# Two graph layers on one core: the first graph's queries as seven products, lead-in copies on VectorE, row sums made with the column sums

## The chip, the cores and the metric

The kernel runs on one core of a Trainium2 chip. The core has a matrix engine (TensorE, PE in the profile), two elementwise engines (VectorE, DVE; ScalarE, ACT), GpSimd (POOL) and SyncE (SP), which here only issues transfers. All data is fp32. The metric is the device time of one launch in microseconds; less is better.

## The reference, cut to what matters

`x` is 16 graphs of 1024 nodes with 256 channels; `adj` is one 1024 x 1024 matrix for all of them. Layer 0, for each graph, with `h = relu(layernorm(x))`:

```python
fea = transpose(h, (0, 2, 1))                    # 256 x 1024
c_adj = mean(fea, axis=1)                        # one number per node
diff = c_adj[:, None, :] - c_adj[:, :, None]
A = abs(abs(sigmoid(diff) - 0.5) - 0.5) * 2.0
Wg = adj * (A + transpose(A)) * 0.5
q = relu((fea @ Wg) * para)                      # "queries", 256 x 1024
k, v = split(h @ kv_w)
x = x + softmax(q k / sqrt(64)) v                # 4 heads
```

Layer 1 takes the sums of the adjacency with the identity added, by rows and by columns, less the diagonal:

```python
deg = sum(A_norm, axis=0) + sum(A_norm, axis=1) - diagonal(A_norm)
A_hat = A_norm * rsqrt(deg)[:, None] * rsqrt(deg)[None, :]
```

It multiplies all graphs with `A_hat` and sends them through two linear layers with batch norms over all graphs.

## The kernel before, in words

**Stages.** A lead-in makes the first graph's keys, values and queries. Then one attention after another runs, of graphs 0 to 15, and each has the next graph's preparation (keys, values, queries) and the earlier graph's layer 1 woven into it as background. A second stage with the second linear layer ends the launch. Every engine does its instructions in the order in which the program lists them: a schedule written out by hand. `weave` (L151) takes a main generator and lets side generators go one step with each of its steps, from a given step on, and runs the sides out after it. `double` (L161) takes two slots of a generator at once. `attention` (L1240) runs 16 steps per graph: the scores of a step are issued (`scores`), ACT takes their Exp (L1089), DVE adds them up (L1113), PE multiplies the step before with the values (L1124), and background steps follow until a budget of PE time is used up. The scores have two PSUM tiles, so PE's next scores wait for the Exps of the last ones.

**Weighting.** `weigh` (L477) makes the weighted adjacency `Wg` in eight tiles of 128 x 1024, each half a row of a 2 x 4 pattern: column half `q`, pair of row blocks `th`. A tile takes two ACT operations (Abs, L508), a third (Tanh, L516) and one on DVE with the adjacency tile (L495). The generator has 17 slots, two per tile, and loads the adjacency one tile ahead into a ring of three buffers (tag "adj"). For graph 0 alone, DVE also reduces each adjacency tile by rows into `rows` (L498), since the sums by rows are needed in layer 1.

**Queries.** `plain_queries` (L638) multiplies all blocks: 32 products of 128 x 128 x 512 in 16 steps, each step two products. It ends each of its four output quarters with one multiplication by `para` (L663) on DVE and a Relu on ACT (L666). `queries` (L537), used for graphs 2 and later, splits both factors into 2 x 2 blocks of quarters and needs seven products of quarters instead of eight (14 steps). For that DVE makes sums and differences: two on the graph's own `h` (`combine`, L534 and L535) and two later (L580, L581), eight on weighted tiles in place (`take`, L571), and nine additions of products out of PSUM (L579 to L605); ACT copies the first product twice. The last quarter is multiplied by `para` two deferrals after the seventh product; `para` tiles have two buffers.

**Keys and values.** `keys_values` (L672) has four steps for keys and four for values; ACT copies each product out of PSUM (L683, L700). `transposed` (L412) turns `h` on PE; ACT copies the result (L430). Three PSUM banks rotate among all of these. `differences` (L456) makes the row of column sums `cbc`: for graph 0 DVE spreads the sums (`columns_of`, L205, L210), PE transposes them and ACT copies them (`broadcast_row`, L216, L222).

**Degrees.** `degrees` (L233) runs in the first attention's background. It first reduces `rows`, then goes over eight strips of the transposed adjacency (128 x 1024, loaded by SP at L226, two ahead, in the same ring "adj"): ACT copies a strip in place and sums it (L241), DVE picks its diagonal (L243, L244). `background(0)` (L964) weaves the steps of graph 1's queries with the weighting from step 0 on, graph 2's norm from 4, the building of seven matrices for layer 1 on GpSimd (`graph`) from 5, and `degrees` from 7.

**The lead-in's end** (L1340 on): transposes and two key products, then the second half of the transposes, `differences(0)`, the other six steps of keys and values with six slots of the weighting, the load of graph 1, the queries of graph 0 with one slot of weighting for each step and graph 1's norm from step 5 on, and the attention.

Of the kernel before, what the change touches and what calls it, by code (L numbers as in the profile page):

```python
# [10 lines left out]
F32 = mybir.dt.float32  # L11
AF = mybir.ActivationFunctionType
ALU = mybir.AluOpType
AX = mybir.AxisListType
# [3 lines left out]
P = 128  # L18
# [5 lines left out]
def gnn_two_layers_kernel(  # L24
# [12 lines left out]
    nc = tc.nc  # L37
    B, N, C = x.shape
    H1 = w1_t.shape[1]
    NT = N // P  # L40
# [3 lines left out]
    FB = 512  # L44
    NH = N // FB
    TH = 2
    NP = NT // TH
# [7 lines left out]
    ident = const.tile([P, P], F32, name="ident")  # L55
# [43 lines left out]
    def layers(shifted):  # L99
# [8 lines left out]
        big = st.enter_context(tc.tile_pool(name=f"big_{kind}", bufs=1))  # L108
        p1 = st.enter_context(tc.tile_pool(name=f"p1_{kind}", bufs=1))
        p2 = st.enter_context(tc.tile_pool(name=f"p2_{kind}", bufs=2))  # L110
        p3 = st.enter_context(tc.tile_pool(name=f"p3_{kind}", bufs=3))
# [11 lines left out]
        xs, hs, hts, ats, qs, ks, vs = {}, {}, {}, {}, {}, {}, {}  # L123
# [20 lines left out]
        def run(*parts):  # L144
            for part in parts:
                while advance(part) is not None:
                    pass
            while queue:
                queue.pop(0)()

        def weave(main, *sides):  # L151

            for i, cost in enumerate(main):
                for start, side in sides:
                    if i >= start:
                        cost += next(side, 0.0)
                yield cost
            for _, side in sides:
                yield from side

        def double(slots):  # L161

            for _ in slots:
                next(slots, None)
                yield 0.0
# [34 lines left out]
        load_x(0)  # L200
        kvw = const.tile([P, CC, 2 * C], F32, tag="kvw", name=f"kvw_{kind}")
        nc.sync.dma_start(out=kvw, in_=kv_w.rearrange("(k p) j -> p k j", p=P))
        rows = big.tile([P, NH, NT], F32, name="rows")

        def columns_of(col, name):  # L205

# [6 lines left out]
                cbs.append(cb)  # L213
            return cbs

        def broadcast_row(dst, cbs, name):  # L216

            for g, cb in enumerate(cbs):
                pt = bank(f"cbp_{name}_{g}")
                for j in range(4):  # L220
                    nc.tensor.transpose(pt[:, j * P : (j + 1) * P], cb[:, j, :], ident)
                nc.scalar.copy(dst[:, g * FB : (g + 1) * FB], pt)  # L222

        def load_adj_t(t, name):
            tile_ = p3.tile([P, N], F32, tag="adj", name=f"{name}_{t}")
            nc.sync.dma_start(out=tile_, in_=adj_t[t * P : (t + 1) * P, :])  # L226
            return tile_

        deg_sm = big.tile([P, 6, NT], F32, name="deg")
        later = {}  # L230
# [1 line left out]

        def degrees():  # L233

            nc.vector.tensor_reduce(row, rows.rearrange("p q t -> p t q"), AX.X, ALU.add)
            ahead = [load_adj_t(t, "at") for t in range(2)]
            yield 0.0
            for t in range(NT):
                a = ahead[t]
                blk = a[:, t * P : (t + 1) * P]  # L240
                nc.scalar.activation(a, a, AF.Copy, accum_out=col[:, t : t + 1])  # L241
                db = p1.tile([P, P], F32, tag="s1", name=f"db_{t}")
                nc.vector.tensor_mul(db, blk, ident)  # L243
                nc.vector.tensor_reduce(diag[:, t : t + 1], db, AX.X, ALU.add)  # L244
                if t + 2 < NT:
                    ahead.append(load_adj_t(t + 2, "at"))
                yield 0.0
            nc.vector.tensor_add(deg, col, row)
            nc.vector.tensor_sub(deg, deg, diag)
            rsqrt(dinv, deg, 1.0, tmp_deg)  # L250
# [161 lines left out]
        def transposed(b, ks, halves=range(NH), meanwhile=None):  # L412

            h = hs["a", b]
            for k in ks:
                if 0 in halves:
                    ht = p3.tile([P, N], F32, tag="ht", name=f"ht_{b}_{k}")
                    hts.setdefault(b, []).append(ht)
            for g in halves:
                pts = [bank(f"htp_{b}_{k}_{g}") for k in ks]  # L420
                for j in range(FB // P):
                    t = g * (FB // P) + j
                    for k, pt in zip(ks, pts):
                        nc.tensor.transpose(
                            pt[:, j * P : (j + 1) * P], h[:, t, k * P : (k + 1) * P], ident
                        )
                    if meanwhile is not None:
                        meanwhile()
                for k, pt in zip(ks, pts):
                    nc.scalar.copy(hts[b][k][:, g * FB : (g + 1) * FB], pt)  # L430

        def squares(b):

# [43 lines left out]
        def weigh(b):  # L477


            csum, cbc = csums[b], cbcs[b]  # L480
            made = weighted[b] = []
            adjs = []

            def load():
                q, th = divmod(len(adjs), NP)
                adjs.append(load_adj(q, th, f"adj_{b}_{q}_{th}"))

            load()
            for slot in range(2 * NH * NP + 1):
                i, odd = divmod(slot, 2)  # L490
                q, th = divmod(i, NP)
                if not odd and i > 0:

                    w, a = made[i - 1], adjs[i - 1]
                    nc.vector.scalar_tensor_tensor(w, w, 1.0, a, op0=ALU.add, op1=ALU.mult)  # L495
                    if b == 0:
                        q, th = divmod(i - 1, NP)
                        nc.vector.tensor_reduce(  # L498
                            rows[:, q, th * TH : (th + 1) * TH], a, AX.X, ALU.add
                        )  # L500
                if not odd and i < NH * NP:
                    q, th = divmod(i, NP)
                    if i + 1 < NH * NP:
                        load()
                    w = p8.tile([P, TH, FB], F32, tag="w", name=f"w_{b}_{q}_{th}")
                    made.append(w)
                    for t in range(TH):
                        nc.scalar.activation(  # L508
                            w[:, t, :].rearrange("p (t q) -> p t q", q=P),
                            cbc[:, q * NT // NH : (q + 1) * NT // NH],  # L510
                            AF.Abs,
                            bias=csum[:, th * TH + t : th * TH + t + 1],
                            scale=-1.0,
                        )
                if odd:
                    nc.scalar.activation(made[i], made[i], AF.Tanh, scale=-0.5 / C)  # L516
                yield 0.0

        AHEAD = 6
# [152 lines left out]
        def keys_values(b):  # L672
            ht = hts[b]
            ks[b] = [p4.tile([P, N], F32, tag="k", name=f"k_{b}_{k}") for k in range(CC)]
            for g in range(NH):
                for j in range(CC):
                    cols = slice(g * FB, (g + 1) * FB)
                    pk = bank(f"pk_{b}_{j}_{g}")
                    for k in range(CC):
                        product(  # L680
                            pk, kvw[:, k, j * P : (j + 1) * P], ht[k][:, cols], k == 0, k == CC - 1
                        )
                    nc.scalar.copy(ks[b][j][:, cols], pk)  # L683
                    yield 1.71

            vs[b] = [p4.tile([P, NT, P], F32, tag="v", name=f"v_{b}_{k}") for k in range(CC)]
            for g in range(NT // 2):
                pv = bank(f"pv_{b}_{g}").rearrange("p (j c) -> p j c", j=2)
                for j in range(2):
                    t = 2 * g + j  # L690
                    for k in range(CC):
                        product(
                            pv[:, j, :],
                            ht[k][:, t * P : (t + 1) * P],
                            kvw[:, k, C : 2 * C],
                            k == 0,
                            k == CC - 1,
                        )
                for k in range(CC):
                    nc.scalar.copy(  # L700
                        vs[b][k][:, 2 * g : 2 * g + 2, :], pv[:, :, k * P : (k + 1) * P]
                    )
                yield 1.71
# [260 lines left out]
        def background(b):  # L964

            if b == 0:
                differences(1)
                for k in range(CC):
# [8 lines left out]
                    (0, w),  # L977
                    (4, norm),
                    (5, islice(build, 8)),
                    (7, islice(sums, 6)),  # L980
                )
                differences(2)
                yield from weave(asked, (0, build), (0, sums))
# [328 lines left out]
        with st:  # L1312
# [22 lines left out]
            else:  # L1335
# [20 lines left out]
                run(islice(products, 2))  # L1356
                transposed(0, range(CC), (1,))
                differences(0)
                run(weave(products, (0, islice(weighers[0], AHEAD))))
                load_x(1, True)  # L1360
                run(weave(plain_queries(0), (0, weighers[0]), (5, Norm(1, True).all())))
                load_x(2, True)
                attention()
                attn.close()
# [348 lines left out]
```

## Time and profile before

| | |
|---|---|
| time, median of 3 runs | 2460.47 us (2459.99 to 2460.54) |
| the profiled execution | 2460.34 us |
| its span | 2458.6 us, granted clock 0.993 |
| busy in the span | PE 98%, DVE 82%, ACT 51%, POOL 23% |
| weighting, per tile | ACT 2 x 0.716 and 1.06 us, DVE 1.22 us |
| rows of the adjacency, L498 | 8 x 1.213 us on DVE |
| k copies L683, v copies L700, ACT | 0.58 us, 0.377 us each |
| strips, L241, ACT | 8 x 1.05 us, and 0.19 us for the sum |

A timeline row has the start, the length, the engine, the line, the operation, out<-in, shapes, a count, and in brackets how long the engine was idle before it and who released it. A table of stretches has each engine's busy time with its number of instructions. A wait table has who waited for whom. PE's instructions come in pairs for each product of 64 columns; a step of 1.71 us shows as eight of them.

### The profile page before, as it was taken

The numbers are of one execution on the slowest core, as the hardware profiler recorded it, in microseconds if no ns is written. First come the engines' busy times: TensorE is split into PE (matmuls) and PEld (weight loads), VectorE is DVE, ScalarE is ACT, GpSimd is POOL, SyncE is SP. The second block draws the span as 40 slices with busy tenths as digits, with TensorE's granted clock in tenths as the row PEclk, the third lists the DMA queues.
The fourth block names the chain that finished last, engine by engine and source line by source line (L and its number), as shares of the span: only waits on it lengthen the run. The fifth ranks groups of instructions, "written<-read, shape, count | busy, mean of one in ns | idle before, by whom it ended". The sixth has DMA issues, their size and how long they took to land. (4 is left out here: it accounts for less than half of the span.)

```text
span 2458.6 us, 35932 instructions
## 1 busy us (share of the span) xinstructions
PE 2412.4 (98%) x13290; PEld 832.6 (34%) x13290; DVE 2003.9 (82%) x3103; ACT 1257.7 (51%) x1870; POOL 559.5 (23%) x645
## 2 busy tenths in 40 slices
PE   9999999999999999999999999999999999999994
PEld 4333333333333333333333333333333332334444
DVE  5678888988888888888898888888888878767775
ACT  7874554545464545445454546454454534335554
POOL 1381202111111212020211212121202103136652
PEclk9999999999999999999999999999999999999997
DMA  4675545363645554453536355544545353456559
GB/s 146 204 242 182 172 138 179 118 229 125 209 139 193 171 189 163 158 171 126 209 117 231 120 201 160 197 164 167 172 134 188 116 201 142 152 197 230 196 193 372
DMA packets 204553, 437.18 MB, mean 178 GB/s; under 512 B 21456, under 2 KB 96720, under 8 KB 200272
## 3 DMA queue, kind: packets, MB, share of 16 engines
q1 hardware_dynamic: 173328, 327.29, 39.7%
q0 software_dynamic: 31040, 107.50, 11.6%
q8 instruction: 107, 1.75, 0.3%
q14 instruction: 78, 0.64, 0.1%
HBM read 331.36 MB, written 103.35 MB: 177 GB/s over the span
## 5 line engine op out<-in xcount | busy, mean ns | idle before, releaser
L1089 ACT ACTIVATE p<-sc 128x1024 f32<-128x1024 f32 x512 | 495.4, 1020 | 649.5 <-PE sc L1081 649.5
L1113 DVE TENSOR_TENSOR acc<-acc,p 128x1024 f32<-128x1024 f32 x384 | 469.8, 1223 | 58.2 <-ACT p L1089 36.9
L1081 PE MATMUL sc<-q,k 64*64 64x512 f32 x4096 | 498.6, 602 | 0.5 <-ACT p L1089 0.5
L1124 PE MATMUL o<-p,v 128*64 128x512 f32 x2048 | 494.7, 604 | 0.0
L174 PE MATMUL pa<-aht,h_b 128*64 128x512 f32 x1536 | 346.0, 592 | 1.1 <-ACT h_b L368 1.1
L174 PE MATMUL pg<-w,x_h 128*64 128x512 f32 x1472 | 332.0, 592 | 0.0
L1081 PEld LDWEIGHTS sc<-q,k 64*64 64x64 f32 x4096 | 131.5, 132 | 336.4 <-issue 287.8
L1124 PEld LDWEIGHTS o<-p,v 128*64 128x64 f32 x2048 | 124.6, 136 | 297.7 <-issue 251.2
L1142 POOL DMA_DIRECT2D out_d<-os x58 | 32.9, 568 | 803.2 <-DVE os L1138 803.2
L495 DVE SCALAR_TENSOR_TENSOR w<-w,adj 128x1024 f32<-128x1024 f32 x128 | 164.9, 1288 | 46.1 <-ACT w L516 45.1
L174 PEld LDWEIGHTS pa<-aht,h_b 128*64 128x64 f32 x1536 | 110.1, 137 | 220.6 <-issue 207.8
L174 PEld LDWEIGHTS pg<-w,x_h 128*64 128x64 f32 x1472 | 105.7, 137 | 210.1 <-issue 198.4
L508 ACT ACTIVATE w<-cbc,csum 128x512 f32<-128x512 f32 x256 | 170.3, 716 | 0.0
L516 ACT ACTIVATE w<-w 128x1024 f32<-128x1024 f32 x128 | 135.6, 1059 | 2.5
L571 DVE TENSOR_TENSOR w<-w,w 128x1024 f32<-128x1024 f32 x112 | 134.6, 1232 | 1.5
L174 PE MATMUL pv<-kvw_f,ht 128*64 128x256 f32 x1024 | 116.1, 379 | 0.0
L174 PE MATMUL pk<-ht,kvw_f 128*64 128x512 f32 x512 | 115.2, 593 | 0.2 <-ACT ht L430 0.2
L174 PE MATMUL py<-at,w 128*64 128x512 f32 x464 | 112.6, 593 | 0.8 <-DVE at L729 0.7
L174 PE MATMUL py<-at,w1s 128*64 128x512 f32 x448 | 107.9, 595 | 0.0
L1453 ACT ACTIVATE yin_f<-yin_f,sm_f 128x512 f32<-128x512 f32 x128 | 93.5, 803 | 19.0 <-DMA yin_f<-y_d 17.0
L826 POOL DMA_DIRECT2D y_d<-y x112 | 61.6, 550 | 145.1 <-DVE y L846 75.8
L1160 DVE TENSOR_REDUCE part<-acc 128x16 f32<-128x512 f32 x128 | 87.8, 686 | 4.4
(197 smaller groups left out, 2968.6 us busy)
## 6 DMA issues: line engine op xcount, KB each, us to landing
aht<-aht_d SPq DMA_DIRECT2D x224, 512.0 KB
adj<-in_adj_dram SPq DMA_DIRECT2D x128, 512.0 KB
y_d<-y POOLq DMA_DIRECT2D x128, 256.0 KB, 3.0
yin_f<-y_d SPq DMA_DIRECT2D x32, 1024.0 KB
para<-in_para_dram SPq DMA_DIRECT2D x64, 256.0 KB
x_d<-x_x POOLq DMA_DIRECT2D x16, 1024.0 KB, 5.1
xo_f<-x_d SPq DMA_DIRECT2D x32, 512.0 KB
out_dram<-xo_f POOLq DMA_DIRECT2D x32, 512.0 KB, 11.1
```

The source lines that it names most:

```text
L174: nc.tensor.matmul(dst[r], left[:, r], right, start=start, stop=stop)
L495: nc.vector.scalar_tensor_tensor(w, w, 1.0, a, op0=ALU.add, op1=ALU.mult)
L508: nc.scalar.activation(w[:, t, :].rearrange("p (t q) -> p t q", q=P), cbc[:, q * NT // NH : (q + 1) * NT // NH], AF.Abs, bias=csum[:, th * ...
L516: nc.scalar.activation(made[i], made[i], AF.Tanh, scale=-0.5 / C)
L571: nc.vector.tensor_sub(block(i)[part], block(x)[part], block(y)[part])
L826: nc.gpsimd.dma_start(out=y1_d[i][:, j, :], in_=y)
L1081: nc.tensor.matmul(sc[part, e, :], ks[b][k][r, m * P + c * HW : m * P + (c + 1) * HW], qs[b][k][r, f * FB : (f + 1) * FB], start=True, sto ...
L1089: nc.scalar.activation(pr, sc, AF.Exp)
L1113: nc.vector.tensor_add(self.acc, self.acc, pr)
L1124: nc.tensor.matmul(self.o[r, :], vs[b][k][:, m, r], pr[:, e, :], start=(m == 0), stop=(m == NT - 1),)
L1160: nc.vector.tensor_reduce(self.part[:, e, :], acc.rearrange("p (c s) -> p c s", s=SQ), AX.X, ALU.add)
L1453: nc.scalar.activation(y, y, AF.Relu, bias=sh[:, j : j + 1], scale=scale[:, j : j + 1])
```

## The change

Four things, in one diff. The first graph's queries use `queries` instead of `plain_queries`, with the weighting two slots ahead at a time, and ten of its slots beside the steps of keys and values. For graph 0 the copies of keys and values, of the second half of the transposes, and of the row `cbc` go to DVE. The reduction of the adjacency by rows leaves `weigh`. In its place `degrees` goes over eight strips of the adjacency itself, then over the eight of its transpose, and starts at step 2 instead of 7.

```diff
-        rows = big.tile([P, NH, NT], F32, name="rows")
...
+        def copier(b):
+
+            return nc.vector.tensor_copy if b == 0 else nc.scalar.copy
+
         def broadcast_row(dst, cbs, name):
 
             for g, cb in enumerate(cbs):
                 pt = bank(f"cbp_{name}_{g}")
                 for j in range(4):
                     nc.tensor.transpose(pt[:, j * P : (j + 1) * P], cb[:, j, :], ident)
-                nc.scalar.copy(dst[:, g * FB : (g + 1) * FB], pt)
-
-        def load_adj_t(t, name):
-            tile_ = p3.tile([P, N], F32, tag="adj", name=f"{name}_{t}")
-            nc.sync.dma_start(out=tile_, in_=adj_t[t * P : (t + 1) * P, :])
-            return tile_
+                nc.vector.tensor_copy(dst[:, g * FB : (g + 1) * FB], pt)
+
+        def load_strip(u):
+            strip = p3.tile([P, N], F32, tag="adj", name=f"strip_{u}")
+            t = u % NT
+            nc.sync.dma_start(
+                out=strip, in_=(adj if u < NT else adj_t)[t * P : (t + 1) * P, :]
+            )
+            return strip
...
         def degrees():
 
-            nc.vector.tensor_reduce(row, rows.rearrange("p q t -> p t q"), AX.X, ALU.add)
-            ahead = [load_adj_t(t, "at") for t in range(2)]
+            ahead = [load_strip(u) for u in range(2)]
             yield 0.0
-            for t in range(NT):
-                a = ahead[t]
-                blk = a[:, t * P : (t + 1) * P]
-                nc.scalar.activation(a, a, AF.Copy, accum_out=col[:, t : t + 1])
-                db = p1.tile([P, P], F32, tag="s1", name=f"db_{t}")
-                nc.vector.tensor_mul(db, blk, ident)
-                nc.vector.tensor_reduce(diag[:, t : t + 1], db, AX.X, ALU.add)
-                if t + 2 < NT:
-                    ahead.append(load_adj_t(t + 2, "at"))
+            for u in range(2 * NT):
+                t, a = u % NT, ahead[u]
+                into = row if u < NT else col
+                nc.scalar.activation(a, a, AF.Copy, accum_out=into[:, t : t + 1])
+                if u >= NT:
+                    db = p1.tile([P, P], F32, tag="s1", name=f"db_{t}")
+                    nc.vector.tensor_mul(db, a[:, t * P : (t + 1) * P], ident)
+                    nc.vector.tensor_reduce(diag[:, t : t + 1], db, AX.X, ALU.add)
+                if u + 2 < 2 * NT:
+                    ahead.append(load_strip(u + 2))
                 yield 0.0
...
-                    nc.scalar.copy(hts[b][k][:, g * FB : (g + 1) * FB], pt)
+                    (nc.vector.tensor_copy if g > b else nc.scalar.copy)(hts[b][k][:, g * FB : (g + 1) * FB], pt)
...
                     nc.vector.scalar_tensor_tensor(w, w, 1.0, a, op0=ALU.add, op1=ALU.mult)
-                    if b == 0:
-                        q, th = divmod(i - 1, NP)
-                        nc.vector.tensor_reduce(
-                            rows[:, q, th * TH : (th + 1) * TH], a, AX.X, ALU.add
-                        )
...
-                    nc.scalar.copy(ks[b][j][:, cols], pk)
+                    copier(b)(ks[b][j][:, cols], pk)
...
-                    nc.scalar.copy(
+                    copier(b)(
                         vs[b][k][:, 2 * g : 2 * g + 2, :], pv[:, :, k * P : (k + 1) * P]
                     )
...
-                    (7, islice(sums, 6)),
+                    (2, islice(sums, 11)),
...
-                run(weave(products, (0, islice(weighers[0], AHEAD))))
+                run(weave(products, (0, double(islice(weighers[0], 10)))))
                 load_x(1, True)
-                run(weave(plain_queries(0), (0, weighers[0]), (5, Norm(1, True).all())))
+                run(weave(queries(0), (0, double(weighers[0])), (5, Norm(1, True).all())))
```

## The prediction

> **What bounds the kernel now.** I read the page first, then a table of stretches, then the timeline around the end of the lead-in.
>
> ```profile
> PE 2412.4 (98%) x13290; PEld 832.6 (34%) x13290; DVE 2003.9 (82%) x3103; ACT 1257.7 (51%) x1870; POOL 559.5 (23%) x645
> ```
>
> PE is busy for nearly the whole span, so I asked where it is not, and how full the others are in the stretches that the change touches (columns: stretch, then busy us and instructions of each engine, clock, DMA share, GB/s):
>
> ```profile
> core 0: us, PE busy (x) PEld busy (x) DVE busy (x) ACT busy (x) POOL busy (x), PEclk, DMA share, GB/s
> ...
> 16.00:26.50 10.50, 10.50 (x82) 5.80 (x82) 3.90 (x4) 9.08 (x18) 0.00 (x0) 1.00 0.18 35
> 26.50:54.10 27.60, 27.60 (x133) 9.07 (x129) 20.45 (x34) 19.84 (x38) 2.60 (x5) 1.00 0.47 159
> 54.10:74.70 20.60, 20.11 (x123) 6.97 (x121) 9.17 (x9) 14.96 (x22) 0.00 (x0) 1.00 0.55 173
> ...
> 110.00:130.00 20.00, 20.00 (x120) 6.16 (x116) 16.43 (x26) 13.92 (x25) 18.54 (x23) 1.00 0.89 293
> ```
>
> The lead-in is PE's from 16 to 54 us: no gap. But DVE already fills 20.5 of the 27.6 us of the first queries. The hand-over to the first attention, from the timeline:
>
> ```profile
> 54.09 1.95 PE L1081 MATMUL sc<-q,k 64*64 64x512 f32 x16
> 54.20 0.69 DVE L663 TENSOR_TENSOR q<-pg,para 128x512 f32<-128x512 f32 x1 [1.02 <-PE pg L174]
> ...
> 54.93 0.63 ACT L666 ACTIVATE q<-q 128x512 f32<-128x512 f32 x1 [1.09 <-DVE q L663]
> 55.47 1.92 ACT L1089 ACTIVATE p<-sc 128x1024 f32<-128x1024 f32 x2
> ...
> 56.52 2.00 PE L1081 MATMUL sc<-q,k 64*64 64x512 f32 x16 [0.49 <-ACT p L1089]
> ```
>
> The last queries' product ends near 54.1; its multiplication (DVE), its Relu (ACT) and only then the first Exp follow in ACT's order, and PE's second scores wait for that Exp: 0.49 us, the only gap that the waits of PE show between 54 and 175 us. Behind 56.52 PE never waits in that attention, so what the lead-in gains or loses reaches the end whole. The mark to watch is the start of the second scores, 56.52.
>
> DVE's price list comes from a later graph, whose queries already are seven products:
>
> ```profile
> 186.35 1.22 DVE L495 SCALAR_TENSOR_TENSOR w<-w,adj 128x1024 f32<-128x1024 f32 x1
> 187.48 0.69 DVE L579 TENSOR_TENSOR q<-pg,q 128x512 f32<-128x512 f32 x1
> 188.08 0.68 DVE L580 TENSOR_TENSOR x_h<-s_a,x_h 128x512 f32<-128x512 f32 x1
> 188.80 0.69 DVE L581 TENSOR_TENSOR x_h<-x_h 128x512 f32<-128x512 f32 x1
> ```
>
> Start to start, a full queue takes 1.14 us for 1024 elements, 0.60 for 512, 0.72 where an operation reads what the one before wrote. In the same way a pair of row statistics (L344 x2, L346 x2) takes 0.87.
>
> **What the Trainium skill says.** "VectorE: DVE Perf Modes", the perf-mode tier table: an fp32 tensor_tensor runs at 1x, and so does fp32 with an operand in PSUM. The trace agrees: 1.23 us for 1024, 0.69 for 512. The errata section of that page prices a PSUM-to-SBUF operation at 120 cycles plus one per element at 0.96 GHz; for the PSUM copies, which this trace doesn't have on DVE, that is an estimate of 0.66 us (512) and 0.39 (256); I use the spacing 0.60 of L579 and 0.33, the spacing of L344 at 256. "TensorE: Matmul & The Clock Gate", the section on array and queue depths, says that ACT and DVE are strict FIFO, so an operation behind a wait waits too. Part 1 of that page says that after about 3.4 us of idleness the clock drops to half. The trace shows it once, after PE's last product at 2382.09:
>
> ```profile
> 2384.00:2385.00 1.00, 0.00 (x0) 1.00 0.97 397
> ...
> 2386.00:2387.00 1.00, 0.00 (x0) 0.50 1.04 422
> ...
> 2391.00:2392.00 1.00, 1.00 (x6) 0.51 0.00 0
> 2392.00:2393.00 1.00, 1.00 (x8) 1.00 0.81 250
> ```
>
> **The change part by part.**
>
> *Products.* 16 steps of 1.71 us (27.6 us) become 14: PE loses 3.4 us of work. This is the whole prize.
>
> *Copies.* ACT is relieved of 4 k copies (0.58), 8 v copies (0.38), 2 ht (0.59), 2 cbc (0.61): 7.7 us, so a weighted tile takes ACT 1.33 + 1.06, start to start 2.31 us, with nothing between. DVE gets them. A wait comes with that: DVE's column copies (L210), which ran at 9.84 and 13.10 in an idle DVE, now stand behind the second k copy (14.0) and the two ht copies (from 14.90, 0.60 each). They run at 16.1 and 16.45, and PE's cbp transposes, next in its order, end near 17.8 instead of 16.2. PE starts the third k product at 17.8 instead of 16.13: 1.65 us given back. Tile 0's Abs can start near 18.05.
>
> *Row reductions.* 8 x 1.14 = 9.1 us leave DVE. *Quarters.* They bring combine 1.3, eight takes (L571) 9.1, two more steps on h 1.3, nine additions 5.4; four multiplications stay. With 12 us of k and v copies, ht, cbc (4 x 0.6 + 8 x 0.33 + 4 x 0.6 = 7.4) DVE gains 24.5 and loses 9.1: 15 us more, on top of 24.35 in 38 us.
>
> So I run DVE's queue in program order. From 22.0: first weighting (L495, 1.14), then in turn two v copies (0.66) and a weighting, to 28.5 after the fourth; v copies to 29.2; combine to 30.5; fifth weighting, take, sixth weighting, take: 35.1. Seventh weighting: its Tanh ends at 20.5 + 6 x 2.31 plus 1.1 for ACT's two copies of the first product = 35.4. From there DVE has no idle time: weighting 36.5; addition and two steps on h 38.5; last weighting 39.6; multiplication, addition 40.8; take 41.9; statistics 42.8; two takes 45.1; statistics, addition, statistics and shift 47.5; two takes 49.8; statistics 50.7; two additions, shift 52.25; take 53.4; three additions 55.2. PE alone would have ended near 52 (28.1 + 14 x 1.71); it waits for a12 and for takes, and its last two steps, on the tile taken at 53.4, end at 55.2.
>
> *The last quarter.* Two multiplications start at 55.2 and 55.8. The para tile for the last quarter reuses the buffer that the first of them frees (two buffers), so its load is issued at 55.9. This exact pattern is in the trace once, where DVE waits for it:
>
> ```profile
> 1970.43 1.26 DVE L557 TENSOR_TENSOR q<-q,para 128x512 f32<-128x512 f32 x2
> 1971.12 0.35 SPq L551 DMA_DIRECT2D para<-in_para_dram  x1
> ...
> 1974.50 0.69 DVE L557 TENSOR_TENSOR q<-q,para 128x512 f32<-128x512 f32 x1 [1.54 <-DMA para<-in_para_dram]
> ```
>
> 3.38 us from issue to use. The seventh product's addition is done at 57.1, the multiplication starts at 59.3, ends at 60.0. Behind it on DVE stand the first acc additions; the Relu waits for it, and the Exps behind the Relu. As before (54.89 to 55.47 to 56.52) Exp starts 0.6 later and PE's second scores 1.05 after that: 61.6. Against 56.52: **+5.1 us**. Bounds: +3.8, if copies and spacing are 3% cheaper and para takes the 2.95 us of the first x load (1.18 to 4.13); +6.5, with the copies at full 0.66 and 0.39 and an adjacency load 0.8 late, as one was at 34.14 (1.07).
>
> *Sums in the first attention.* 16 strips instead of 8 and eight more 512 KB loads on SP, in the same ring of three buffers as the weighted tiles' adjacency; ACT pays 1.15 (1.05 + 0.19, overlapped) for each, 9.2 us. In the attention's steps of 7.2 us ACT then has 1.94 of Exp, 2.4 of weighting and 2.3 of two strips: it fits. Exps can come some 4 us late without PE waiting: those of the scores at 74.70 ran at 80.37 without a PE gap. The risk is a load, since ACT stands behind it:
>
> ```profile
> 135.57 1.06 ACT L241 ACTIVATE at<-at 128x1024 f32<-128x1024 f32 x1 [3.08 <-DMA at<-in_adj_t_dram]
> ```
>
> That was the last strip, in the stretch where DMA is 0.89 busy; it cost PE nothing. Now four strips stand there in one attention step. Their loads queue on SP behind the column sums' cbc, the last behind the use of the strip three before. I put ACT's Exps near 143 (shifted clock left out) instead of 138.2; the next scores start at 144.5. So 0 to +5, and I take +0.4.
>
> *The rest:* one reduction of rows (0.14) goes; diagonals move along with the second eight strips; later graphs keep ACT's copies. Nothing after the first attention changes.
>
> Sum: +5.1 + 0.4 = +5.5 on the profiled 2460.34 (span 2458.6 and 1.74 around it), 2465.8; the median of the runs is 0.13 above that execution, so **2466.0**.
>
> **The rivals.** *More on top (25%).* PE would idle from 57.2 to 61.6, 4.4 us. The drop above came 3.3 us after the last product and half clock then lasted 4.7 us after work resumed; here that costs 1.7 to 3. Or the last strips stop PE for 2 to 5. Total +7 to +10, 2468 to 2470.5; against it: the gap may fall across two windows, and ACT's slack. *Not slower (20%).* DVE keeps up with PE: if its work behind the weighting is at most 1.71 us a step (I have 27.9 us in 14 steps, 23.9 allowed), PE ends near 52.0, and the second scores start near 54.5 to 55.3, a gain of 1.2 to 2.1: 2459. For it: PE has no gaps today, so less PE work shows at once; against it: no row above is short enough by 15%. *In between (15%).* Fewer waits on DVE and para hidden: -1 to +3.8, 2461 to 2464.
>
> **The numbers.** Forecast 40%, own range 2464.2 to 2467.2. The range that holds all but about a tenth on either side: 2458.3 to 2470. A measurement of this kernel can tell about 0.2% (4.9 us) from no change. Slower by more than that: three fifths of the forecast and all of the first rival, 49%. Faster by more would need more than the 3.4 us removed: 2%. Within: 49%.
>
> **What would show it.** PE's third k product near 17.8; DVE without gaps from 35 to 55; PE waiting for DVE takes (L571) and a12 (L581); DVE waiting about 2 us for para before the last multiplication; second scores near 61.6. I am wrong if DVE idles in the queries, if scores start before 55, or if PE gaps past 110 us exceed 1 us.

## The result, and the profile after

| kernel | median of its runs | ratio to before, 95% interval |
|---|---|---|
| before | 2460.38 us (2459.89 to 2460.55) | 1 |
| changed | 2482.84 us (2482.29 to 2484.36) | 1.0093 (1.0080 to 1.0106) |

The changed kernel is 22.5 us slower; 5.5 were forecast. The profiled execution of the changed kernel took 2484.36 us with a span of 2482.6; it was the slowest of its six, 1.5 above the median, so the marks below add up to 24.0 and not to 22.5. Its first page line against that of before: PE has 16 instructions less in the records and 3.9 us more busy time, so it is less work at a lower clock, and the rest of the 24 us is waiting.

```profile
PE 2416.3 (97%) x13274; PEld 832.9 (34%) x13274; DVE 2022.5 (81%) x3131; ACT 1261.4 (51%) x1872; POOL 553.5 (22%) x645
```

The table of stretches (columns as before: stretch, busy time and instructions of each engine, clock, DMA share, GB/s) tells where. Before the change PE was busy 27.60, 20.11 and 20.00 us in the first three of these stretches and 10.00 in each of the last three, at a clock of 1.00 in all six:

```profile
26.50:54.10 27.60, 24.15 (x114) 9.14 (x112) 24.30 (x43) 14.12 (x24) 1.26 (x2) 0.94 0.44 143
54.10:74.70 20.60, 15.40 (x90) 5.46 (x85) 10.99 (x16) 10.88 (x19) 1.35 (x3) 0.83 0.39 115
110.00:130.00 20.00, 17.08 (x98) 5.21 (x96) 15.09 (x23) 14.75 (x28) 17.92 (x22) 1.00 0.79 266
140.00:150.00 10.00, 10.00 (x64) 3.54 (x62) 9.72 (x15) 4.82 (x7) 8.93 (x13) 1.00 0.61 191
150.00:160.00 10.00, 6.75 (x52) 2.73 (x48) 5.17 (x9) 3.63 (x7) 4.89 (x8) 1.00 0.99 363
160.00:170.00 10.00, 7.29 (x36) 2.85 (x38) 6.96 (x12) 9.62 (x18) 8.20 (x14) 0.66 0.96 340
```

There are holes in the lead-in, in its hand-over and in the middle of the attention, and stretches at a lower clock. PE's wait table over the first 250 us names them (who waited for whom, total, times, longest):

```profile
PE sc L1082 <- ACT p L1090: 6.8, 2, 4.2
PE pv L174 <- ACT v L701: 6.0, 1, 6.0
PE pg L174 <- DVE h_a L582: 3.5, 1, 3.5
PE cbp_c L224 <- DVE cb_c L209: 1.7, 1, 1.7
```

I mark the starts of PE's scores one after another, in both traces. The difference between the two kernels grows at five marks, and once more behind the last scores:

| scores | before | changed | later by | what happened since the mark above |
|---|---|---|---|---|
| second | 56.52 | 64.89 | 8.37 | lead-in |
| third | 61.34 | 72.00 | 10.66 | clock at half |
| fourth to eighth | | | 10.65 to 10.66 | nothing |
| ninth | 108.99 | 122.85 | 13.86 | a strip's load |
| tenth to thirteenth | | | 13.92 | nothing |
| fourteenth | 144.48 | 166.31 | 21.83 | the last four strips' loads, and 1.8 of half clock behind them |
| fifteenth | 148.23 | 171.25 | 23.02 | clock at half again |
| the last | 2122.70 | 2145.89 | 23.19 | nothing of size |
| end of the span | 2458.6 | 2482.6 | 24.0 | waits in the last stage, not followed here |

**The lead-in's end**, from the timeline of the changed kernel. The last scores before the gap are those at 58.74; DVE waits for `para`, PE for the Exp:

```profile
38.65 1.22 DVE L501 SCALAR_TENSOR_TENSOR w<-w,adj 128x1024 f32<-128x1024 f32 x1 [2.81 <-DMA adj<-in_adj_dram]
...
58.74 1.95 PE L1082 MATMUL sc<-q,k 64*64 64x512 f32 x16
...
59.24 0.33 SPq L552 DMA_DIRECT2D para<-in_para_dram  x1
...
62.57 0.69 DVE L558 TENSOR_TENSOR q<-q,para 128x512 f32<-128x512 f32 x1 [2.15 <-DMA para<-in_para_dram]
63.29 0.63 ACT L560 ACTIVATE q<-q 128x512 f32<-128x512 f32 x1 [2.81 <-DVE q L558]
63.83 1.92 ACT L1090 ACTIVATE p<-sc 128x1024 f32<-128x1024 f32 x2
64.89 1.99 PE L1082 MATMUL sc<-q,k 64*64 64x512 f32 x8 [4.20 <-ACT p L1090]
```

The first row is the one that the forecast hadn't: the seventh weighting waits 2.81 us for its adjacency tile. PE stands still from 60.69 to 64.89, and the granted clock is at half from 62.96 to 69.78 (worked out from stretches of 1 us, two of which follow):

```profile
63.00:64.00 1.00, 0.00 (x0) 0.50 1.06 364
...
69.00:70.00 1.00, 1.00 (x7) 0.61 0.01 1
```

**The ninth scores.** Here ACT stands before one of the first eight strips, whose load went out at 116.37:

```profile
120.22 1.06 ACT L246 ACTIVATE strip<-strip 128x1024 f32<-128x1024 f32 x1 [2.93 <-DMA strip<-in_adj_dram]
...
122.85 2.00 PE L1082 MATMUL sc<-q,k 64*64 64x512 f32 x16 [2.64 <-ACT p L1090]
```

**The last four strips**, SP's queue first, then ACT, then PE:

```profile
142.46 1.81 SPq L475 DMA_DIRECT2D csum_d<-csumt  x4
146.81 0.34 SPq L479 DMA_DIRECT2D cbc<-csum_d  x1
147.25 9.53 SPq L230 DMA_DIRECT2D strip<-in_adj_t_dram  x4
```

```profile
154.95 1.06 ACT L246 ACTIVATE strip<-strip 128x1024 f32<-128x1024 f32 x1 [8.54 <-DMA strip<-in_adj_t_dram]
...
157.34 1.06 ACT L246 ACTIVATE strip<-strip 128x1024 f32<-128x1024 f32 x1 [0.72 <-DMA strip<-in_adj_t_dram]
...
159.71 1.06 ACT L246 ACTIVATE strip<-strip 128x1024 f32<-128x1024 f32 x1 [0.70 <-DMA strip<-in_adj_t_dram]
...
162.03 0.63 ACT L701 COPY v<-pv 128x256 f32<-128x256 f32 x2
```

```profile
162.71 3.68 PE L174 MATMUL pv<-kvw_f,ht 128*64 128x256 f32 x16 [5.96 <-ACT v L701]
```

The reader should follow one chain. SP had last issued a strip at 136.49 and then stood at `csum_d`, because DVE's transpose of the column sums ran only at 142.23, behind additions of the attention and diagonals of strips. The strips' loads stand behind that in SP's order, so the first of the four starts at 147.25. The transfer engines are 0.32 and 0.47 busy in the two microseconds from 147 on, and full from 149 on (0.99 in 150 to 160); the strip is used at 154.95. ACT waits in its order in front of that strip; its copies of `v`, which have nothing to do with the strips, stand behind all four. PE's next product waits for the PSUM bank that a `v` copy has to empty.

### The profile page after: what moved, and what is told of

The parts are those of the page before. It is cut to its first block, busy times and chain, and to the rows that moved or that the text cites. A ratio compares the mean times of both kernels' runs of the same rounds, so it can differ in the third digit from the quotient of the medians.

```text
span 2482.6 us, 35950 instructions
## 1 busy us (share of the span) xinstructions
PE 2416.3 (97%) x13274; PEld 832.9 (34%) x13274; DVE 2022.5 (81%) x3131; ACT 1261.4 (51%) x1872; POOL 553.5 (22%) x645
## 5 line engine op out<-in xcount | busy, mean ns | idle before, releaser
L572 DVE TENSOR_TENSOR w<-w,w 128x1024 f32<-128x1024 f32 x120 | 144.0, 1229 | 1.7
L174 PEld LDWEIGHTS pv<-kvw_f,ht 128*64 128x64 f32 x1024 | 74.1, 138 | 58.1 <-issue 19.3
```

Source lines behind the costliest of these rows:

```text
L174: nc.tensor.matmul(dst[r], left[:, r], right, start=start, stop=stop)
L572: nc.vector.tensor_sub(block(i)[part], block(x)[part], block(y)[part])
```

## The experiments

Each run is given with its median and its ratio to runs of the kernel before on the same chip (2460.11 to 2460.67 in four sets of runs). "Second" and "third" are the scores' starts in its profiled execution.

**One half each.** Does the loss come from the lead-in, the strips, or from both together? `strips_only` is the kernel before with the parts of the diff above on `rows`, `load_strip` and `degrees`, and with `degrees` from step 2; `leadin_only` is the changed kernel with this:

```diff
-            for u in range(2 * NT):
-                t, a = u % NT, ahead[u]
-                into = row if u < NT else col
+            for u in range(NT):
+                t, a, into = u, ahead[u], col
...
-            nc.vector.tensor_add(deg, col, row)
+            nc.vector.tensor_add(deg, col, col)
...
-                    (2, islice(sums, 11)),
+                    (7, islice(sums, 6)),
```

> The kernel before with only the degrees part of the change: the row reductions leave the weighting, 16 strips run in the first attention from step 2. Theory A (the strips themselves stop ACT, whose Exps and copies then come late, and PE stands): the second scores stay at 56.5 us, and the time rises by 10 to 13 us, to 2470.5 to 2473.5. Rival B (the strips only hurt because the lead-in hands over late and ACT starts the attention behind): at most 2 us over the kernel before.

> The changed kernel without the eight row strips and with the degrees at their old place (the sums by rows are left out; the column sums stand in for them). Theory A: the lead-in part alone: second scores near 64.9 us, then half clock, third scores 10.7 us late, and nothing more: 2471 to 2472. Rival B: the same lead-in, but the delays behind 110 us belong to the lead-in as well: 2480 or more.

Strips alone: 2470.85, 1.0045 (1.0029 to 1.0062), so +10.5. Lead-in alone: 2470.05, 1.0041 (1.0027 to 1.0055), so +9.7. In the first, the second scores are at 56.42, as before, and the losses are at the ninth scores (111.85 against 108.99) and the fourteenth (154.68 against 144.48). In the second, the scores are 9.4 late from the third on (70.70), and nothing is lost behind that. Theory A holds in both, except that `leadin_only` is 1 us faster than it said: its clock was at half for 3.4 us, not for 6.8. The two add up to 20.3 of 22.5.

**Is it ACT's work on the strips, or their loads?** `strips_twice` gives ACT the same 16 passes at the same steps, over eight loaded strips:

```diff
             for u in range(2 * NT):
-                t, a = u % NT, ahead[u]
-                into = row if u < NT else col
+                t, a = u // 2, ahead[u // 2]
+                into = row if u % 2 == 0 else col
...
-                if u + 2 < 2 * NT:
-                    ahead.append(load_strip(u + 2))
+                if u % 2 and t + 2 < NT:
+                    ahead.append(load_strip(t + 2))
```

> The kernel before with the degrees' part of the change, except that ACT goes twice over each of the eight strips of the transposed adjacency instead of once over each of sixteen strips: as many ACT passes, at the same steps, and no load more than in the kernel before. What it leaves out: the sums by rows (column sums stand in). The full part alone took 2470.9 against 2460.3. Theory A (the loss is the landing of eight more 512 KB loads, which ACT stands behind): no wait of PE for Exps or v copies of more than 1 us, the thirteenth scores within 1 us of 144.5, 2460 to 2462. Theory B (the loss is ACT's 9 us of further passes, or their place): the thirteenth scores stay some 10 us late, 2468 to 2471.

2463.03, 1.0012 (1.0006 to 1.0019): +2.7, between the two but near A. The time is above A's 2462, and one wait for an Exp was 1.9 us where A allowed 1, so A holds only in the main. PE waits for no `v` copy; the fourteenth scores (called the thirteenth in the expectation) are at 146.91, 2.43 late, and 2.37 of that is there at the ninth, ahead of which ACT stood 4.1 us before a strip. The trace puts this wait down to a DVE operation on another tile; the strip's own load went out at 104.96 and the pass began at 108.73, so it is probably a load's landing as well. DMA share in 140 to 150 is 0.99 here too. So 7.8 of the 10.5 are the eight further loads, and 2.7 what is left without them, the earlier start included; the time of ACT's passes by itself shows at no mark.

**Moving the late load.** Could the strips be put ahead of the column sums? `sums_first` issues `differences(2)` behind the last strips:

```diff
-                differences(2)
                 yield from weave(asked, (0, build), (0, sums))
+                differences(2)
```

> The changed kernel with the column sums' row for graph 2 (a transpose, four small writes and a broadcast load on SP) put behind the last strips instead of ahead of them. Theory A (the last four strips land late because their loads stand on SP behind that broadcast, issued at 147 us): the 8.5 us wait of ACT and the 6 us gap of PE go, nearly all of 9: 2474 to 2476. Rival (the transfer engines are full there, 0.9 and more, and a strip takes its 7.7 us from wherever it starts; the loads also wait for the ring's buffers): 1 to 3 us less, 2480 to 2482.

2484.5, 1.0097 (1.0080 to 1.0113): no gain, so Theory A falls, and the rival's gain of 1 to 3 us didn't come either. ACT's waits before the last four strips shrink from 10.0 us to 4.8, and the next piece in SP's queue inherits what was gained. ACT now stands at the first Abs of graph 2, which needs `cbc`:

```profile
165.37 1.33 ACT L509 ACTIVATE w<-cbc,csum 128x512 f32<-128x512 f32 x2 [5.89 <-DMA cbc<-csum_d]
```

PE's wait for `v` is 2.0 (6.0 above), and its waits for Exps 11.3 (6.8 above). What is last in the queue is late, whichever it is. With `strips_twice`, whose eight loads less take away most of the loss, this says that the loads are too many for these 15 us, not only wrongly ordered. No run moves the loads of GpSimd's matrices out of these 15 us, so their share in it is not shown.

**Without strips.** `rows_graph1` keeps the lead-in, and makes the row sums on DVE as the kernel before did, but beside graph 1's weighting, where DVE has room:

```diff
                     nc.vector.scalar_tensor_tensor(w, w, 1.0, a, op0=ALU.add, op1=ALU.mult)
+                    if b == 1:
+                        q, th = divmod(i - 1, NP)
+                        nc.vector.tensor_reduce(
+                            rows[:, q, th * TH : (th + 1) * TH], a, AX.X, ALU.add
+                        )
```

> The changed kernel with no row strips: the sums by rows are reduced by DVE beside graph 1's weighting, and the column strips stand where they stood before. Theory A (strips cost 10 to 12 us, and DVE has room in the first attention for 8 reductions of 1.14 us): as the lead-in alone, 2470 to 2471. Rival (any work for the row sums in the first attention costs about as much): 2478 or more.

2471.74, 1.0046 (1.0030 to 1.0063), 11.1 less than the changed kernel; no wait of PE behind the lead-in. A holds in its mechanism; the time is 0.7 above its upper number. (The column strips are back at step 7 here, as in the kernel before.)

**The lead-in's three terms.** One edit each on the changed kernel. `x_later` issues graph 1's load three steps later, so that it no longer shares the transfer engines with the adjacency tile; `para_early` gives the last `para` tile a buffer that is free earlier; `keep_awake` lets PE do 24 transposes of the identity between the first and the second scores (the edit of the last run below, with 24 for 14).

```diff
-                load_x(1, True)
-                run(weave(queries(0), (0, double(weighers[0])), (5, Norm(1, True).all())))
+                asked, w = queries(0), double(weighers[0])
+                run(weave(islice(asked, 3), (0, islice(w, 3))))
+                load_x(1, True)
+                run(weave(asked, (0, w), (2, Norm(1, True).all())))
```

```diff
-                paras[k, q] = p2.tile([P, FB], F32, tag="para", name=f"para_{b}_{k}_{q}")
+                own = b == 0 and (k, q) == (1, 0)
+                paras[k, q] = p2.tile(
+                    [P, FB], F32, tag="os" if own else "para", name=f"para_{b}_{k}_{q}"
+                )
...
                 load_para(1, 1)
+                if b == 0:
+                    load_para(1, 0)
...
-                soon(lambda: load_para(1, 0))
+                if b > 0:
+                    soon(lambda: load_para(1, 0))
```

> The changed kernel with graph 1's load issued three query steps later, behind the last two adjacency loads. Theory A (the seventh adjacency tile landed late, at 38.6 us, because a megabyte of x and a para tile stood ahead of it on the transfer engines): seventh weighting near 35.5 instead of 38.65, second scores 3 us earlier, time 2479 to 2480. Rival (the load is late because it waits for its buffer): no change, 2482.8.

> The changed kernel with the last quarter's para tile of graph 0 in a buffer of its own, loaded with the one before. Theory A (the wait for para holds the Exps 2.15 us, and a PE gap of 2 us no longer drops the clock): second scores near 62.7, third near 67.5, 4.5 us earlier; time 2478 to 2479. Rival (only the wait goes, the clock still drops): 2480.7.

> The changed kernel with 24 idle transposes of the identity on PE in its gap between the first and the second scores. Theory A (the gap drops the clock to half until 69.6 us, and the work behind it is bound by PE): third scores at 69.7 instead of 72.0, time 2.3 us less, 2480.5. Rival (Exps and copies on ACT bound that stretch, not PE): no change, 2482.8.

| run | median | ratio, 95% interval | second | third |
|---|---|---|---|---|
| changed | 2482.84 | 1.0093 (1.0080 to 1.0106) | 64.89 | 72.00 |
| x_later | 2480.43 | 1.0080 (1.0063 to 1.0097) | 62.07 | 68.47 |
| para_early | 2477.86 | 1.0072 (1.0056 to 1.0089) | 61.65 | 66.47 |
| keep_awake | 2479.34 | 1.0077 (1.0060 to 1.0094) | 65.83 | 70.66 |

The seventh weighting is at 36.02 in `x_later` (38.65 above), and the second scores follow, 2.82 earlier. `para_early` brings them 3.24 earlier; 1.12 of that was there before the wait for `para`, at the first scores (57.62 against 58.74). Its PE gap is 2.08 us, the clock stays at 1.00, and the third scores are 5.53 earlier. In `keep_awake` third scores come 4.83 behind the second ones, as in the kernel before (4.82), against 7.11 in the changed kernel: the clock stayed at 1.0. The times of the three fall by 2.4, 5.0 and 3.5 us. They don't simply follow the third scores, since the stop at the last strips differs from run to run: PE's wait for `v` was 7.2 in `x_later`, and the expected 2479 to 2480 was missed by 0.4. Theory A holds in its mechanism in all three; `para_early` and `keep_awake` came 0.1 and 1.2 us under the times that it said.

**All of it together, and GpSimd.** `lighter` has the row sums beside graph 1, `para_early` and `x_later`, the spread of the column sums ahead of the second k copy, and `ht` copied by ACT. And it gives GpSimd some of DVE's queue:

```diff
-                run(islice(products, 2))
+                run(islice(products, 1))
+                early.extend(columns_of(csums[0], "c0"))
+                run(islice(products, 1))
...
-                    (nc.vector.tensor_copy if g > b else nc.scalar.copy)(hts[b][k][:, g * FB : (g + 1) * FB], pt)
+                    nc.scalar.copy(hts[b][k][:, g * FB : (g + 1) * FB], pt)
...
-            combine("a", b, nc.vector)
+            combine("a", b, nc.vector if b > 0 else nc.gpsimd)
...
-                nc.vector.tensor_sub(block(i)[part], block(x)[part], block(y)[part])
+                by = nc.gpsimd if b == 0 and part == 1 else nc.vector
+                by.tensor_sub(block(i)[part], block(x)[part], block(y)[part])
...
-                nc.vector.tensor_sub(a11, s1, a11)
-                nc.vector.tensor_sub(a12, a12, a11)
+                by = nc.gpsimd if b == 0 else nc.vector
+                by.tensor_sub(a11, s1, a11)
+                by.tensor_sub(a12, a12, a11)
```

> The changed kernel with DVE relieved: row sums beside graph 1's weighting, column copies ahead of the second key product, the second half's ht copies on ACT, the sums of quarters and half of the takes of graph 0 on GpSimd, the last para tile early, x of graph 1 after the adjacency. Theory A (the lead-in is bound by DVE's queue and what it waits for; freed of that it is bound by PE, which has 3.4 us less to do): second scores near 53.5, 2457 to 2458, faster than the kernel before. Rival (GpSimd's subtractions slow DVE or come late): second scores at 57 or later, 2461 or more.

2467.76, 1.0027 (1.0017 to 1.0038): the rival held, with second scores at 61.89. My ledger for two engines (a ledger is the list of an engine's instructions with the time that each ends) was wrong. Two rows of `lighter`'s timeline show one reason:

```profile
47.78 2.35 POOL L583 TENSOR_TENSOR w<-w,w 128x1024 f32<-128x1024 f32 x1
47.84 2.30 DVE L364 SCALAR_TENSOR_TENSOR lnsm_a<-mv_a,lnsm_a 128x4 f32<-128x4 f32 x1
```

A DVE operation on four elements, 0.16 us elsewhere (L363 at 50.74 in the changed kernel), lasts as long as GpSimd's. Six of DVE's operations between 34 and 56 us are stretched so, by 8.4 us in all against the same operations in the changed kernel. Another reason is GpSimd's own pace: it takes 2.35 us for a subtraction that takes DVE 1.23, and PE waits 2.5 for the quarter that GpSimd makes. The runs don't split the two. So I took GpSimd out again (`no_pool`), and then also gave the eight `v` copies to ACT (`no_pool_v`):

```diff
-                    copier(b)(
+                    nc.scalar.copy(
                         vs[b][k][:, 2 * g : 2 * g + 2, :], pv[:, :, k * P : (k + 1) * P]
                     )
```

> The changed kernel with row sums on DVE beside graph 1's weighting, the last para tile in a buffer of its own, graph 1's load three steps later, the spread of the column sums ahead of the second k copy, and the second half of the transposes copied by ACT: the run called lighter without its use of GpSimd. Lighter took 2467.8 with second scores at 61.9. Theory A (there GpSimd's and DVE's operations held each other up, and what is left is DVE's full queue): without GpSimd DVE has no operation of over 2 us, the ledger ends near 51.5, second scores at 57.5 to 59, 2461 to 2464. Theory B (GpSimd's share of the work was a net help): second scores at 62 to 64 and 2467 to 2470.

> As no_pool, and ACT makes the copies of the first graph's values (8 x 0.38 us) instead of DVE. Theory A (DVE's queue sets the lead-in's end, and ACT has room): DVE's ledger is 2.6 us shorter, so PE is bounded by its own 14 steps; second scores at 55 to 56.5, 2459 to 2461, no slower than before. Theory B (ACT's Abs and Tanh of the first tiles are late instead, and DVE waits for them): second scores no earlier than in no_pool.

`no_pool`: 2462.40, 1.0008 (1.0000 to 1.0017), second scores at 57.81; A held in both numbers. `no_pool_v`: 2465.73, 1.0021 (1.0014 to 1.0029), second scores at 60.45; B held, and A falls. ACT is on the way of the weighted tiles, and each pair of `v` copies makes a tile come 0.5 to 1.2 us later, so that DVE waits for tiles five times, 4.7 us in all; in `no_pool` it never does. Two of the rows of `no_pool_v`, and the same last weighting in `no_pool`, where it starts 2.64 earlier:

```profile
24.46 1.23 DVE L503 SCALAR_TENSOR_TENSOR w<-w,adj 128x1024 f32<-128x1024 f32 x1 [1.76 <-ACT w L524]
...
39.38 1.22 DVE L503 SCALAR_TENSOR_TENSOR w<-w,adj 128x1024 f32<-128x1024 f32 x1
```

```profile
36.74 1.22 DVE L503 SCALAR_TENSOR_TENSOR w<-w,adj 128x1024 f32<-128x1024 f32 x1
```

The lead-in with seven products is therefore held in `no_pool` by DVE's full queue, with ACT's eight tiles (done at 35.7) so little ahead that the `v` copies on ACT make them the later of the two; the copies lie better on DVE. The last run adds 14 transposes of the identity to `no_pool`, whose third scores were 6.42 behind the second:

```diff
                     made = scores(*unit.at, g)
+                    if s == 0 and not shifted:
+                        rest = bank("rest")
+                        for i in range(14):
+                            nc.tensor.transpose(
+                                rest[:, i % NS * P : (i % NS + 1) * P], ident, ident
+                            )
```

> The run called no_pool, and 14 idle transposes on PE between the first and the second scores, where PE stood for 2.1 us and the granted clock was then 0.50 from 58 to 60 us and 0.65 from 60 to 62. No_pool took 2462.4 against 2460.3, with third scores 6.42 us behind the second ones where the kernel before has 4.82. Theory A (the half clock comes from PE standing still after a queries stage that already had short waits): the spacing returns to 4.8, third scores at 62.6 to 62.9, 2460.5 to 2461.3, which is level with before. Theory B (the drop has another cause, such as the load of DVE and ACT at that point): the spacing stays at 6.4 and the time at 2462 to 2463.

2461.76, 1.0006 (0.9998 to 1.0015). Third scores are 4.83 behind the second, at 62.85, as A says; the time is 0.5 above A's. The medians differ by 0.6, within both intervals, and not by the 1.6 of the scores, for the profiled execution of `no_pool` (2463.79) was its slowest of 12, nine of which lie between 2461.7 and 2462.7. The drop seems to come in some of them only. No profile here shows that, but the mean clocks fit it: the six fastest of the 12 (up to 2462.24) had 0.993, the other six 0.992, and all 13 executions with the transposes 0.993. No version beat the kernel before; this one can't be told from it.

## Why the prediction was wrong

*The sign and the lead-in's mechanism were right.* DVE's ledger was close: cbp waits 1.70, third k product at 17.63 (17.8 said), Abs of tile 0 at 18.08 (18.05), the take after the sixth weighting ends near 35.7 (35.1). From the seventh weighting to the end DVE has one gap of 0.3 us, where the forecast had none. PE waited for a12 (3.45) and for takes (1.0). DVE waited 2.15 us for `para` (about 2 said), and from its issue at 59.24 to the multiplication at 62.57 it took 3.33 (3.38 taken). `leadin_only` and `para_early` confirm this part. (The "12 us" of copies in the forecast is a slip; its sum uses the right 7.4.)

*First wrong step: "Seventh weighting: its Tanh ends at ... = 35.4".* I asked for ACT's release only. The weighting also needs its adjacency tile. In the changed order 1 MB of graph 1's `x` is issued at 27.19 and `para` at 28.25, ahead of this tile's load at 29.02. The weighting came at 38.65, 3.25 later than the ledger had it. My upper bound named such a wait, at 0.8 us, from one in the kernel before. `x_later` gives back 2.63 of it at the weighting and 2.82 at the second scores. The Trainium skill, "DMA: Bandwidth & Descriptors", section "Issuing engines are not separate DMA queues", says that transfers run on the same 16 transfer engines and interleave, whichever engine issued them. Here SP issued them all, and the trace agrees: from 31 to 37 the engines are full (a share of 1.05), and with `x` behind the tile the weighting is 2.63 earlier. I hadn't applied it to this load.

*Second: the clock.* I had it as a rival, at 1.7 to 3, and at nothing in the sum; it came, at 2.3, and `keep_awake` removes it. So the lead-in cost 5.1 + 3.3 + 2.3 = 10.7 in the profiled execution (10.66 at the third scores) and 9.7 as the median of `leadin_only`.

*Third and largest: "So 0 to +5, and I take +0.4".* The term is mis-sized: the strips cost 10.5 by themselves. The forecast's own sign of being wrong, PE gaps past 110 us of more than 1 us, came with 2.64 and 5.96. Its first rival had named the clock or the strips (2 to 5), as alternatives; both came, and the strips at more than twice that. I had the right place (four strips in one step, their loads behind `cbc` on SP) but priced ACT's passes: Exps near 143. What stands there is landing time. From the first issue (147.25) to the first use (154.95) passed 7.7 us, and then one 512 KB strip came each 2.4 us, since in 147 to 160 the transfer engines moved 4.1 MB, 1.5 of it for the matrices that GpSimd builds. Some 3 us of the 10.5 are lost earlier, at the ninth scores, where I had nothing: "it fits" counted ACT's work, and ACT stood 2.93 us before a strip. `strips_twice` shows that the passes are the small part, if any, and `sums_first` that the order of these loads only chooses who waits. A second error lies beside it: the row of 3.08 us that "cost PE nothing" was the only strip behind `cbc` then. It was issued at 128.21 and used at 135.57, so a landing time of up to 7.4 us stood in the trace of before. Now four strips stand there, with waits of 8.54, 0.72 and 0.70 before three of them, and `cbc` itself is issued at 146.81 instead of 127.76 (13.9 of the 19 is the lateness that all had by then).

*What is not split.* The halves sum to 20.3, the whole to 22.5. Part of the 2.2 is the clock: it was at half for 6.8 us in both places of the changed kernel, and for 3.4 us in each half alone. In the profiles that is 0.7 more at the third scores, and the 1.2 of the fifteenth, which `strips_only` doesn't have; the rest I haven't separated.

*The prize.* The 3.4 us of PE work did go, but PE doesn't set the lead-in's end any more. With the load, the `para` tile, the strips and the idle clock mended, the seven products are level with the sixteen steps, because DVE's queue ends where PE did, with ACT's tiles close ahead of it.

## What to carry to other kernels

Before moving work to where an engine has room, list what each moved instruction needs: a 512 KB load that an in-order engine stands behind costs its landing time at the transfer engines' load at that moment (up to 7.7 us here), and everything queued behind it pays. In a ledger of an engine's queue, give each entry all its releases, the loads too, not only the last one of the old order. Saved PE work is a gain only while PE is the last to arrive; where other queues end at nearly the same time, count them first.

## What the runs showed of the hardware

- DVE operations waited out GpSimd's. The Trainium skill, "SBUF — State Buffer", section "Who interferes with whom", says that a DVE instruction with two SBUF inputs contends with a GpSimd instruction that reads SBUF, and that the port pair they share is an exclusive lock. The rows of `lighter` agree: 2.30 us for 0.16 beside a GpSimd operation of 2.35. I hadn't applied it to `lighter`.
- The granted clock fell to 0.50 some 2.3 us after PE's last work in the changed kernel (idle from 60.7, 0.73 in the stretch 62.5 to 63.5). A gap of 2.1 us was followed by the drop in the profiles of `lighter`, `no_pool` and `no_pool_v`, and not in that of `para_early`; one of 3.6 us was not in `rows_graph1`. So the length of a gap alone doesn't decide, and the "about 3.4 us of idleness" and the 3.3 us from the kernel's end (3.07 by the granted clocks) that the forecast quoted don't hold as a limit; the measurement decides.
- By the granted clocks of stretches of 1 us, the half clock then lasted 3.4 us in `leadin_only`, `strips_only`, `x_later`, `lighter`, `no_pool` and `no_pool_v`, and 6.8 us, twice as long, at 63 and at 162 us in the changed kernel and at the end of the kernel before. Why once or twice, no run here shows.
- Copies out of PSUM on DVE: 0.69 us for 128 x 512, against the forecast's estimate of 0.66, and 0.66 from start to start for a pair of 128 x 256 (23.07 to 23.73 in the changed kernel), the twice 0.33 that the forecast took.
